# First FFN: down products two slices behind the gated products in all batches; scan: later weight loads, shift and root in steps of their own

## The chip, the cores and the metric

The kernel runs on one core of a Trainium2 chip. The metric is the device time of one launch in microseconds. TensorE (PE, with its weight loads as PEld), VectorE (DVE), ScalarE (ACT), GpSimd (POOL) and the queue of SyncE (SP) work side by side and meet through semaphores.

## The reference

Two blocks of a sequence model, in float32, on four batches of 512 tokens with 512 channels. What the change touches is the first FFN, then the scan of the second block, and the entry of the last attention, of which batch 0 is prepared inside the scan.

```python
x = x + _L0_attn_ref(_layernorm(x), W_qkv, W_o)
x = x + _L0_ffn_ref(_layernorm(x), w1, w3, w2)
x = x + _L1_attn_ref(_layernorm(x), W_xproj, W_dt, b_dt, A_log, D_param)
x = x + _L1_ffn_ref(_layernorm(x), ...)

def _L0_ffn_ref(x, w1, w3, w2):          # w*q: weights rounded to three values
    g = silu(x @ w1q.T) * (x @ w3q.T)    # hidden size 1365
    return g @ w2q.T

def _L1_attn_ref(x, W_xproj, W_dt, b_dt, A_log, D_param):
    ...
    def step(h, inp):                    # 512 tokens, 512 channels, 16 states
        h = dA_t * h + Bu_t
        y = jnp.sum(h * C_t[:, None, :], axis=-1)
        return (h, y)
    ...

def _L1_ffn_ref(x, ...):                 # latent attention, then a mixture of experts
    h = x + attention(rmsnorm(x, ln1_w), kv_d_w, q_d_w, k_u_w, v_u_w, ...)
    return h + moe(rmsnorm(h, ln2_w), ...)
```

## The kernel before

The residual rows stay in SBUF (`xs[b]`, one tile per batch). The stages follow one another: first attention, first FFN, scan, second attention, experts. Two of them matter here.

**First FFN** (the loop over `b` and the 11 slices `f` of the hidden size; the last slice has 85 rows). `gated(b, f, ...)` makes one slice: sixteen matmuls into `pg`, a tile of the PSUM tag "pair" with two buffers of two banks (L844), then silu on ACT (L849), the product with the other half on DVE (L850), a rounded copy `gh` on ACT (L855) and the rest `gl` on DVE (L856). `gh` and `gl` have `GBUFS` = 3 buffers each. `down(b, f, ...)` multiplies a finished slice with `w2` into the four banks `ys` (eight matmuls, L862); the first of a batch begins with the first finished slice that leaves `pending`. After the last slice what is left in `pending` is multiplied, and DVE adds `ys` to `xs[b]` (L914). The list `pending` holds the slices whose down product is not yet issued; it may hold `lag` of them, 2 in batch 0 and 1 in the others.

Between these products the loop calls `part(n)` three times a slice: in the middle of the gated products, after them, and after the down product. In batches 1 to 3 a part advances `prepare(b - 1, ...)`, which makes the scan's inputs of the batch before: layer norm rows (`row_s`, L123), their products on POOL (L590, L591), transposes `tp` into a half of a "pair" buffer with a copy to `uT` on ACT (L132, L133), the projections `pb`, `pd`, `pz`, the softplus on ACT and DVE (L635 to L649), and transposes `tpd` of `ux` (L657). Later parts also advance `inputs(b + 1)`, which makes the next batch's `hTh` and `hTl` through transposes `tpf` (L826 to L833). Parts 2, 3 and 5 advance nothing. Part 0 is the layer norm, part 1 makes rows 0 and 1, part 4 is the transpose of row 0, part 6 that of row 1. In this stage only PE's order is that of the text (`manual_schedule`); the order on DVE, ACT, POOL and SP, and the buffer that a tile takes, are chosen by the framework's planner.

**Scan** (128 steps `m`: batch, state `n`, half). Here the order on all engines is that of the text. A step issues, in this order: DVE's addition of the batch before (`finish`, at `m % 32 == 3`), a part of `between` (the last batch's preparation, drained at `m` = 84), a part of `come` from `m` = 85 on, at even steps `scale` for the next `n` (a `diag` load on SP, three `bu` rows L1103 and four decays `da` L1109 on ACT), the first turn of the next step on PE (L1116, L1121), the two scans on DVE (L1129), `weigh` on POOL (`hc`, L1140, at even steps with a `cb` load on SP, L1137), `add_up` of step `m - 3` on PE (L1153) and the second turn. PSUM has eight banks: four hold the sums `ys`, the turns and the parts share the others.

At `m` = 84 the pool of the last batch's preparation is closed, its room is given to the tiles of the later stages, and a list `loads` is filled: 14 loads on SP and one memset of `wr` on POOL, in the order `ln1`, `wlat` twice, `wrk` (the profile's `w_b`), `wup` three times, `wku`, `cos1`, `sin1`, `wow`, `ln2`, the memset, `wr`, `br`. From `m` = 86 each step issues one. In steps 91 to 94 ACT scales a quarter of `wlat` and of `wrk` by `ln1` (L1248).

`come` is `enter(0, c1, 1)`; its argument `apart` is 1 only here (for the other batches `enter` runs in the second attention with `apart` = 0). A step runs it to its next `yield`. Before the change its parts are: steps 85 to 88 one token slice's statistics each on DVE (L108, L109), in 88 also `root_inverse` (a `tensor_scalar` on DVE, L102, and a power on POOL, L103); step 89 the shift on DVE (L150) and the first shifted row with its square and sum on ACT (L155, L1015); steps 90 to 92 the other three, in 92 also the second `root_inverse`; steps 93 to 98 the rows `row_d` (ACT, L1028), their transposes (PE, L1032) and the copies to `hT` (ACT, L1023); from step 99 `enter_singly`, which begins with the products `pl` of `wlat` and `hT` (L956), two matmuls a step.

Of the kernel before, what the change touches and what calls it, by code (L numbers as in the profile page):

```python
# [22 lines left out]
NK = C // P  # L23
# [6 lines left out]
GBUFS = 3  # L30
# [16 lines left out]
def block_kernel(ctx: ExitStack, tc: tile.TileContext, a: dict, out: bass.AP):  # L47
# [50 lines left out]
    def root_inverse(pool, v, eps, scale, name):  # L98

        shape = list(v.shape)  # L100
        r = pool.tile(shape, F32, tag="ri_" + name, name="ri_" + name)
        nc.vector.tensor_scalar(r, v, scale, eps, ALU.mult, ALU.add)  # L102
        nc.gpsimd.tensor_tensor(r, r, minus_half[:, : shape[1]], ALU.pow)  # L103
        return r
# [42 lines left out]
    def shift_of(pool, mv, rs):  # L147

        shift = pool.tile([P, NT], F32, tag="shift", name="shift")
        nc.vector.scalar_tensor_tensor(shift, mv[:, :, 0], -1.0, rs, ALU.mult, ALU.mult)  # L150
        return shift
# [635 lines left out]
    with tc.tile_pool(name="b_s", bufs=1) as bs, tc.tile_pool(name="b_1", bufs=1) as b1, tc.tile_pool(  # L787
# [3 lines left out]
        def quantize_down(f):  # L791
            rows = FROWS[f]
            raw = b2.tile([P, C], F32, tag="row", name="q_w2")[:rows]
            nc.sync.dma_start(raw, a["w2T"][f * P : f * P + rows, :])
            ternary(b2, w2[:rows, f, :], raw, scales["w2"], C)

        def clear():
            zero = b2.tile([P, C], F32, tag="sil", name="zero")
            nc.vector.memset(zero, 0.0)
            nc.gpsimd.dma_start(acc[B * T :, :], zero)  # L800
# [66 lines left out]
        with tc.manual_schedule(engines={mybir.EngineType.PE}):  # L867
            for _ in inputs(0, first_mv):
                pass
            for f in range(3):  # L870
                quantize_down(f)
            for b in range(B):
                hT = high_low.pop(b)
                between = prepare(b - 1, bs, half_pair, halves, 2) if b > 0 else iter(())
                coming = inputs(b + 1) if b + 1 < B else iter(())
                ys = None

                light = [False]

                def part(n):
                    if n % 3 == 2 and n > 3 * 4 and b + 1 < B:
                        next(coming, None)
                        if not light[0]:
                            return
                    if n not in (2, 3, 5):
                        light[0] = next(between, False)


                lag = GBUFS - 1 if b == 0 else 1
                pending = []
                for f, rows in enumerate(FROWS):
                    pending.append((f, rows, gated(b, f, rows, hT, lambda: part(3 * f))))
                    if b == 0 and f + 3 < NF:
                        quantize_down(f + 3)
                    if b == 0 and f == 6:
                        clear()
                    part(3 * f + 1)  # L900
                    if b == B - 1 and f == 0:
                        for _ in fetch(0):
                            pass
                    if b == 0 and f == 4:
                        scan_constants(b2)
                    if len(pending) > lag:
                        if ys is None:
                            ys = [bank(f"y{t}") for t in range(NT)]
                        down(b, *pending.pop(0), ys)
                    part(3 * f + 2)  # L910
                for job in pending:
                    down(b, *job, ys)
                for t in range(NT):
                    nc.vector.scalar_tensor_tensor(  # L914
                        xs[b][:, t, :], ys[t], scales["w2"][:, 2:3], xs[b][:, t, :], ALU.mult, ALU.add
                    )
# [84 lines left out]
    def enter(b, pool, apart=0):  # L1001


        mv = pool.tile([P, NT, 2], F32, tag="mv", name="mv_d")
        for t in range(NT):
            statistics(pool, xs[b], t, mv)
            if t == NT - 1:
                rs = root_inverse(pool, mv[:, :, 1], LN_EPS, 1.0, "ln")
            yield
        shift = shift_of(pool, mv, rs)  # L1010
        ss = pool.tile([P, NT], F32, tag="ss", name="ss_d")
        for t in range(NT):
            shifted(hs[b][:, t, :], xs[b], t, rs, shift)
            sq = pool.tile([P, C], F32, tag="row", name="sq_d", bufs=2)
            nc.scalar.activation(sq, hs[b][:, t, :], AF.Square, accum_out=ss[:, t : t + 1])  # L1015
            if t == NT - 1:
                rs = root_inverse(pool, ss, RMS_EPS, 1.0 / C, "rms")
            yield
        hT = far.tile([P, NK, T], F32, tag="hT", name="hTd")
        before = tp = None  # L1020
        for t in range(NT + 1 + apart):
            if tp is not None:
                nc.scalar.copy(hT[:, :, (t - 2) * P : (t - 1) * P], tp.rearrange("p (k q) -> p k q", k=NK))  # L1023
                tp = None
            row = None
            if t < NT:
                row = pool.tile([P, C], F32, tag="row", name="row_d", bufs=2)
                nc.scalar.activation(row, hs[b][:, t, :], AF.Copy, scale=rs[:, t : t + 1])  # L1028
            if before is not None and apart:
                tp = bank("tp")  # L1030
                for k in range(NK):
                    nc.tensor.transpose(tp[:, k * P : (k + 1) * P], before[:, k * P : (k + 1) * P], ident)  # L1032
            elif before is not None:
                transpose_into(hT, before, (t - 1) * P)
            before = row
            yield
        if apart:
            yield from enter_singly(b, pool, hT)
            return
        lat = d1.tile([P, 2, T], F32, tag="lat", name="lat")  # L1040
        for i in range(2):
            pl = bank("pl")
            for k in range(NK):
                nc.tensor.matmul(
                    pl, wlat[:, k, i, :], hT[:, k, :], start=k == 0, stop=k == NK - 1
                )
            nc.scalar.copy(lat[:, i, :], pl)
        yield
        v = d2.tile([P, NT, C], F32, tag="v", name="vd")
        both = turned_pair()  # L1050
        rows = {}
        for t in range(NT + 2):
            if t >= 2:
                done = rows.pop(t - 2)
                for s, scale in enumerate((SCALE, 1.0)):
                    transpose_into(
                        both[s], done[:, s].rearrange("p h d -> p (h d)"), (t - 2) * P, scale
                    )
            if t < NT:
                tok = slice(t * P, (t + 1) * P)  # L1060
                pv = bank("pvd")
                nc.tensor.matmul(pv, lat[:, 0, tok], wup[:, 0, :], start=True, stop=True)
                nc.scalar.copy(v[:, t, :], pv)

                pq = pair("pqd")
                nc.tensor.matmul(pq[:, 0, :], lat[:, 1, tok], wup[:, 1, :], start=True, stop=True)
                nc.tensor.matmul(pq[:, 1, 0 : H * RD], lat[:, 0, tok], wku, start=True, stop=True)
                for k in range(NK):
                    nc.tensor.matmul(
                        pq[:, 1, H * RD :], hT[:, k, tok], wrk[:, k, :],  # L1070
                        start=k == 0, stop=k == NK - 1,
                    )
                qk = rows[t] = d2.tile([P, 2, H, D], F32, tag="qk", name="qkd")
                rot = d1.tile([P, 2, H, RD], F32, tag="rot", name="rotd")
                for s in range(2):
                    rotate(qk, rot, pq[:, s, :], t, s)
                nc.gpsimd.tensor_tensor(qk[:, :, :, RD:], qk[:, :, :, RD:], rot, ALU.add)
            if t < NT + 1:
                yield
        ready[b] = both + (v,)  # L1080
        yield

    eight("s")
    with tc.tile_pool(name="c_1", bufs=1, reuse_waits="tile") as c1, tc.tile_pool(
# [83 lines left out]
        with tc.manual_schedule(engines=engines):  # L1168
            coming, loads = iter(()), []
# [3 lines left out]
            for m, (b, n, half) in enumerate(steps):  # L1173
# [27 lines left out]
                if m == 84:  # L1201
# [38 lines left out]
                    loads.append(lambda: nc.gpsimd.memset(wr, 0.0))  # L1240
                    hold(wr[:, :, :NR], by_rows(a["router_w"]))
                    hold(br, a["router_b"].partition_broadcast(P))
                if m >= 86 and loads:
                    loads.pop(0)()
                if 91 <= m < 91 + NK:
                    k = m - 91
                    for w in (wlat[:, k].rearrange("p i r -> p (i r)"), wrk[:, k]):
                        nc.scalar.activation(w, w, AF.Copy, scale=ln1[:, k : k + 1])  # L1248
            for step in steps[-3:]:
# [60 lines left out]
    with tc.tile_pool(name="d_1", bufs=1) as d1, tc.tile_pool(name="d_2", bufs=2) as d2, tc.tile_pool(  # L1310
# [146 lines left out]
        with tc.manual_schedule(engines={mybir.EngineType.PE}):  # L1457
# [5 lines left out]
            for m in range(n + 4):  # L1463
                b, at = divmod(m, each)
# [358 lines left out]
```

## Time and profile before

| | us |
|---|---|
| median of 3 runs | 1855.8 (1854.12 to 1862.17) |
| profiled execution, whole | 1858.7 |
| its span, first to last instruction | 1857.0 |
| first attention | 0 to 428 |
| first FFN | 428 to 733 |
| scan | 733 to 1100 |
| second attention | 1100 to 1535 |
| experts | 1535 to 1857 |

Over the span PE is busy 94%, DVE 64%, ACT 51%, POOL 31%. The mean granted clock of TensorE is 0.98. Busy shares over the whole span mix stages with different limits; the prediction therefore reads one stage at a time. In the lines that it shows, "[x <-Y]" after an instruction is the time for which its engine sat idle before it, and the instruction that ended that wait. Times of lines in the order of time are from the start of the span.

### The profile page before, as it was taken

To read this page: it belongs to the slowest core of one execution; us is meant where nothing else is said; L and a number is where in the kernel's file an instruction comes from. 1 tells how busy PE (TensorE), PEld (TensorE's weight loads), DVE (VectorE), ACT (ScalarE), POOL (GpSimd) and SP (SyncE) were. 2 spreads that over 40 slices of the span, in tenths; PEclk is the share of its full clock that TensorE was granted. 3 is DMA by queue.
4 is the path that set the end of the run, shared out by engine and by line. 5 is a ranking of instruction groups with operands and counts; after the bars stand their busy time and mean duration, and the time that the engine had idled before them with its cause. 6 is when DMAs were issued, how large, how long until landed. Compare 5 with 4: busy or idle time off the path is not lost.

```text
span 1857.0 us, 27575 instructions
## 1 busy us (share of the span) xinstructions
PE 1740.2 (94%) x10374; PEld 1093.0 (59%) x10374; DVE 1186.6 (64%) x1908; ACT 938.0 (51%) x1940; POOL 581.5 (31%) x383
## 2 busy tenths in 40 slices
PE   7899899989999998989997989999999999999998
PEld 3443344437777676878886875556556554544444
DVE  6577757786655556899887886574766764322222
ACT  2433533332242536889988867576676652111111
POOL 2231313120202021889887860100000000244431
PEclk9999999999999999999999988999999999999999
DMA  7002300102011112333223200000010006455545
GB/s 244 22 1 68 109 1 1 46 1 76 5 40 53 59 56 82 94 92 102 58 73 102 58 28 1 1 24 1 1 35 24 24 24 230 150 91 91 91 79 142
DMA packets 74630, 115.07 MB, mean 62 GB/s; under 512 B 9546, under 2 KB 34762, under 8 KB 73940
## 3 DMA queue, kind: packets, MB, share of 16 engines
q1 hardware_dynamic: 64996, 90.87, 15.4%
q0 software_dynamic: 8656, 20.32, 6.1%
q10 hardware_dynamic: 848, 2.13, 0.3%
q8 instruction: 83, 1.36, 0.3%
q14 instruction: 47, 0.39, 0.1%
HBM read 83.02 MB, written 33.42 MB: 63 GB/s over the span
## 4 chain that ended last, share of the span: by engine, by line
PE 68%; DVE 13%; ACT 11%; issue 3%; DMA 3%; POOL 1%; DVEq 0%; SPq 0%; ACTq 0%; POOLq 0%
PE pgr L1702 7%; PE pg L844 6%; PE pq L284 5%; PE ys L1153 4%; PE yr L1723 4%; PE scd L1387 4%; PE bu L1121 3%; PE y L1327 3%; PE y L862 3%; PE pge L1288 3%; PE tp L132 3%; PE bu L1116 3%; PE y L340 3%; PE tpd L1410 2%; ACT pr L1398 2%
## 5 line engine op out<-in xcount | busy, mean ns | idle before, releaser
L1140 POOL TENSOR_TENSOR hc<-h,cb 128x1024 f32<-128x1024 f32 x128 | 301.1, 2378 | 115.4 <-DVE h L1129 93.7
L1129 DVE TENSOR_TENSOR_SCAN h<-da,bu 128x512 f32<-128x512 f32 x256 | 295.1, 1204 | 28.5 <-PE bu L1121 14.3
L284 PE MATMUL pq<-wqkv,hT 128*128 128x512 f32 x384 | 179.6, 615 | 4.8 <-DVE qk L300 3.6
L1109 ACT ACTIVATE da<-delta_l,am 128x511 f32<-128x511 f32 x256 | 163.4, 709 | 2.1 <-DVE h L1129 2.0
L1398 ACT ACTIVATE pr<-scd,nm 128x128 f32<-128x128 f32 (+3 forms) x256 | 133.3, 530 | 57.6 <-DVE nm L1395 56.7
L844 PE MATMUL pg<-hTh,w 128*128 128x512 f32 (+1 forms) x352 | 145.6, 414 | 1.0 <-ACT hTh L831 0.7
L844 PE MATMUL pg<-hTl,w 128*128 128x512 f32 (+1 forms) x352 | 139.9, 397 | 0.2 <-DVE hTl L832 0.2
L1153 PE MATMUL ys<-ident,hc 128*128 128x128 f32 x1024 | 136.7, 277 | 3.3 <-DVE h L1129 1.7
L1121 PE MATMUL bu<-ident,bu 128*128 128x128 f32 x768 | 132.2, 279 | 6.4 <-ACT bu L1103 6.4
L1702 PE MATMUL pgr<-wgu,gTe 128*128 x304 | 137.1, 593 | 0.0
L1103 ACT ACTIVATE bu<-dxT,bts 128x512 f32<-128x512 f32 x192 | 124.3, 712 | 16.2 <-PE bu L1121 13.3
L284 PEld LDWEIGHTS pq<-wqkv,hT 128*128 128x128 f32 x384 | 71.5, 194 | 97.3 <-issue 91.2
L366 ACT ACTIVATE pt<-sc 128x1024 f32<-128x1024 f32 (+3 forms) x128 | 83.3, 698 | 78.0 <-PE sc L361 72.3
L1387 PE MATMUL scd<-kTd,qTd 32*128 32x512 f32 (+3 forms) x512 | 109.0, 507 | 14.0 <-ACT pr L1398 11.3
L1153 PEld LDWEIGHTS ys<-ident,hc 128*128 128x128 f32 x1024 | 119.0, 143 | 4.3 <-DVE h L1129 1.9
L1116 PE MATMUL bu<-diag_l,dxT 128*128 128x128 f32 x512 | 105.9, 289 | 16.3 <-DVE h L1129 13.3
L367 POOL TENSOR_SCALAR_AFFINE_SELECT pt<-pt 128x512 f32<-128x512 f32 x64 | 56.2, 879 | 179.1 <-ACT pt L366 156.5
L1395 DVE TENSOR_REDUCE nm<-scd 128x2 f32<-128x256 f32 (+3 forms) x128 | 105.0, 821 | 2.8
L1410 PE MATMUL tpd<-ident,pr 128*128 128x128 f32 x640 | 102.6, 290 | 3.5 <-ACT ptd L1417 1.1
L1116 PEld LDWEIGHTS bu<-diag_l,dxT 128*128 128x128 f32 x512 | 82.3, 196 | 40.0 <-DVE h L1129 23.2
L1121 PEld LDWEIGHTS bu<-ident,bu 128*128 128x128 f32 x768 | 95.6, 145 | 9.9 <-ACT bu L1103 9.9
L1709 DVE SCALAR_TENSOR_TENSOR hidr<-pgr,silr 128x256 f32<-128x256 f32 x38 | 16.1, 425 | 130.0 <-ACT silr L1707 130.0
(338 smaller groups left out, 3290.7 us busy)
## 6 DMA issues: line engine op xcount, KB each, us to landing
cb<-c_rows SPq DMA_DIRECT2D x64, 256.0 KB, 3.3
q_w<-in_w2T SPq DMA_DIRECT2D x20, 256.0 KB, 2.8
diag_l<-diags SPq DMA_DIRECT2D x64, 64.0 KB, 2.0
hrows<-h SPq DMA_DIRECT2D x4, 1024.0 KB, 4.3
acc<-x SPq DMA_DIRECT2D x16, 256.0 KB, 2.0
wgu<-in_r_gate SPq DMA_DIRECT2D x7, 512.0 KB, 9.5
wgu<-in_r_up SPq DMA_DIRECT2D x7, 512.0 KB, 10.0
wdn<-in_r_down SPq DMA_DIRECT2D x7, 512.0 KB, 9.3
```

The costliest lines, as they stand in the source:

```text
L284: nc.tensor.matmul(y, inputs_T[b][:, k, t * P : (t + 1) * P], wqkv[:, k, s * C : (s + 1) * C], start=k == 0, stop=k == NK - 1,)
L844: nc.tensor.matmul(pg[:rows, i, :], w[:, k, f * P : f * P + rows], part[:, k, :], start=k + m == 0, stop=k + m == NK,)
L1109: nc.scalar.activation(da[:, k, 1:], delta[:, k, 1:], AF.Exp, scale=am[:, k, n : n + 1])
L1116: nc.tensor.matmul(bu[:, :P], loaded[b][1][:, 0, k * P : (k + 1) * P], scaled[b, n][0], start=True, stop=True,)
L1121: nc.tensor.transpose(bu[:, t * P : (t + 1) * P], scaled[b, n][t][:, k * P : (k + 1) * P], ident)
L1129: nc.vector.tensor_tensor_scan(h[:, i, :], decays[b, n][:, 2 * half + i, :], bu, 0.0, ALU.mult, ALU.add)
L1140: nc.gpsimd.tensor_tensor(hc, states.pop((b, n, half)), weighed[b, n].unsqueeze(1).to_broadcast([P, 2, T]), ALU.mult)
L1153: nc.tensor.matmul(sums[b][t][:, k * P : (k + 1) * P], hc[:, i, t * P : (t + 1) * P], ident, is_transpose=True, start=n == 0 and k == 0, s ...
L1387: nc.tensor.matmul(sc[:, i, :w], qT[at, g, t * P : w], kT[at, g, :w], start=True, stop=True)
L1398: nc.scalar.activation(pr[:, i, :w], sc[:, i, :w], AF.Exp, bias=nm[:, i : i + 1], accum_out=sums[b, g][:, t, 2 * p + i : 2 * p + i + 1],)
L1410: nc.tensor.transpose(tp[:, j * P : (j + 1) * P], pr[:, i, j * P : (j + 1) * P], ident)
L1702: nc.tensor.matmul(pg, gT[:, k, :], wgu[:, bass.ds(e, 1), k, :].rearrange("p e o -> p (e o)"), start=k == 0, stop=k == NK - 1,)
```

## The change

In the first FFN `lag` becomes `GBUFS - 1` = 2 in every batch. In `enter`, where `apart` is set, the statistics take two token slices a part, the shift gets a part of its own, and so does the second `root_inverse`; the number of parts stays eight, so `hT`'s rows still begin at step 93. With `apart` = 0 nothing changes. In the scan the loads begin at step 91 instead of 86 and the scalings of `wlat` and `wrk` at 95 instead of 91.

The parts of steps 85 to 92 after the change: two statistics; two statistics and the first root; the shift; four times a shifted row with its square; the second root.

```diff
-                lag = GBUFS - 1 if b == 0 else 1
+                lag = GBUFS - 1
...
             if t == NT - 1:
                 rs = root_inverse(pool, mv[:, :, 1], LN_EPS, 1.0, "ln")
+            if not apart or t % 2 == 1:
+                yield
+        shift = shift_of(pool, mv, rs)
+        if apart:
             yield
-        shift = shift_of(pool, mv, rs)
         ss = pool.tile([P, NT], F32, tag="ss", name="ss_d")
         for t in range(NT):
             shifted(hs[b][:, t, :], xs[b], t, rs, shift)
...
             if t == NT - 1:
+                if apart:
+                    yield
                 rs = root_inverse(pool, ss, RMS_EPS, 1.0 / C, "rms")
             yield
...
-                if m >= 86 and loads:
+                if m >= 91 and loads:
                     loads.pop(0)()
-                if 91 <= m < 91 + NK:
-                    k = m - 91
+                if 95 <= m < 95 + NK:
+                    k = m - 95
```

## The prediction

> **What bounds the kernel now.** I read the stretches of the stages first, then PE's waits in the first FFN, then the order of time on each engine where PE waits. The columns of a stretch are its length, busy time and instructions of PE, weight loads, DVE, ACT and POOL, granted clock, DMA share, GB/s.
>
> ```profile
> 428.00:733.00 305.00, 293.89 (x1356) 222.89 (x1356) 178.50 (x280) 120.62 (x173) 40.20 (x30) 0.99 0.16 51
> 733.00:1100.00 367.00, 336.15 (x2568) 299.09 (x2569) 325.89 (x326) 321.38 (x532) 309.50 (x138) 0.97 0.27 79
> ```
>
> The first row is the first FFN, the second the scan. In the FFN only PE is full: 11.1 of 305 us are idle. In the scan four engines are near their limit; between 1006 and 1099 us PE is busy 91.98 of 93.00. So in both a wait of PE is lost time, unless PE would wait later for the same chain anyway. PE's waits in the FFN (total us, times, longest):
>
> ```profile
> PE y L862 <- DVE gl L856: 4.3, 8, 1.2
> PE y L862 <- ACT gh L855: 2.0, 2, 1.7
> PE tpd L657 <- DVE ux L652: 1.3, 2, 0.7
> ```
>
> The first two, 6.3 us, are what a larger lag can remove. By place: 1.16 and 1.06 at the first down product of batches 1 and 3; 0.30, 0.30, 0.77 in mid-batch; 0.34, 1.87, 0.58 at the last down product of batches 1, 2, 3. The one of batch 2 also costs clock (third figure from the end):
>
> ```profile
> 648.02:651.43 3.41, 1.97 (x7) 1.42 (x8) 1.61 (x3) 1.10 (x2) 0.00 (x0) 1.00 0.85 262
> 651.43:654.84 3.41, 3.41 (x9) 2.64 (x8) 3.41 (x8) 0.00 (x0) 0.00 (x0) 0.50 0.94 320
> ```
>
> PE idles 1.44 us of the first stretch and works at half clock in the second: 1.7 us lost.
>
> **Part 1, lag 2 in batches 1 to 3.** No instruction is added; a down product (eight matmuls, 1.85 us) moves behind the next gated product (sixteen, 3.73 us).
>
> Removed: at the starts 1.16 + 1.06 = 2.2. At the ends down(10) now has two down products ahead of it. gl(10) is ready 3.1, 4.6 and 2.9 us after gated(10), PE comes after some 4, so 0.34 and 0.58 go and 0.5 of 1.87 stays: 2.3. With it goes the half clock, 1.7.
>
> Counted at nothing: the mid-batch 1.37. Behind each, tpd waits for DVE (0.66, 0.67, 1.15) at the end of a chain on ACT and DVE that began earlier; PE only comes there sooner. Without that cover 1.4 more is gained.
>
> Added: down(0) stood between gated(1) and gated(2); now only a transpose (tp) does, and the PSUM pair has two buffers, one held by pg(1), one by tp. In batch 2 gated(1) ends and tp starts at 579.71, and PE is free at 580.06:
>
> ```profile
> 579.97 0.69 ACT L849 ACTIVATE sil<-pg,sc_w 128x512 f32<-128x512 f32 x1 [1.66 <-PE pg L844]
> 580.55 0.59 ACT L133 ACTIVATE uT<-tp 128x512 f32<-128x512 f32 x1
> 581.65 1.62 DVE L123 TENSOR_SCALAR row_s<-x,mv,ri_ln 128x512 f32<-128x512 f32 x1 [1.19 <-POOL ud L590]
> 583.20 0.74 DVE L850 SCALAR_TENSOR_TENSOR sil<-pg,sc_w,sil 128x512 f32<-128x512 f32 x1
> ```
>
> tp's buffer is free at 581.14, pg(1)'s only at 583.94: L850 is queued behind a row that waits for POOL. That a buffer comes free as a whole, after L850, is seen elsewhere; this weight load waits for an L850 that ended at 542.81:
>
> ```profile
> 542.07 0.74 DVE L850 SCALAR_TENSOR_TENSOR sil<-pg,sc_w,sil 128x512 f32<-128x512 f32 x1
> 542.86 0.19 PEld L844 LDWEIGHTS pg<-hTh,w 128*128 128x128 f32 x1 [0.36 <-DVE sil L850]
> ```
>
> Today gated(2) starts at 504.20, 582.26 and 664.32, each time before that L850 ends, so it takes tp's buffer. If it still does, it waits 1.1, 1.15, 1.1; the next transpose, in its middle, takes pg(1)'s buffer and waits 0.7, 0.95, 0.6. Together 5.6. If it takes pg(1)'s instead, 3.7, 3.9, 3.6: 11.2. I take 5.6, since the copy that frees tp's buffer comes first. Each start then has 1.7 to 2.1 us of idle PE within 4 us; a window with 1.44 idle lost the clock, the one from 975.69 with 1.92 did not. Bounds 0 and 3 × 1.7; I take one, 1.7.
>
> The Trainium skill ("TensorE: Matmul & The Clock Gate", section "HAM oscillation") puts the bound at "no PE-idle gaps >~3.4µs". By it the 1.7 that is removed and the 1.7 that is added are both zero, with the same sum here; the trace disagrees at 651.43, where a gap of 1.65 was enough.
>
> Waiting for gh buffers is not added: three buffers, and down(f-3) is issued before gated(f). FFN: -2.2 -2.3 -1.7 +5.6 +1.7 = +1.1.
>
> **Part 2, the scan.** Around steps 85 to 98, the places where an engine waits for another:
>
> ```profile
> 976.85 1.68 DVE L102 TENSOR_SCALAR ri_ln<-mv_d 128x4 f32<-128x4 f32 x1
> 980.85 0.81 ACT L155 ACTIVATE h<-x,shift,ri_ln 128x512 f32<-128x512 f32 x1 [4.02 <-DVE shift L150]
> 991.92 0.17 DVE L102 TENSOR_SCALAR ri_rms<-ss_d 128x4 f32<-128x4 f32 x1 [4.42 <-ACT sq_d L1015]
> 993.27 0.79 PE L1116 MATMUL bu<-diag_l,dxT 128*128 128x128 f32 x2 [3.77 <-DVE h L1129]
> 1005.23 0.66 PE L1032 MATMUL tp<-ident,row_d 128*128 128x128 f32 x4 [2.55 <-ACT row_d L1028]
> ```
>
> ACT, some three steps ahead, stops 4.02 us for the shift, queued on DVE behind scan(88). It is then behind: DVE waits for its fourth square, PE for row_d, and ACT has no pause until 1020.
>
> After the change, DVE, from 966.82: two statistics (0.82 each), scan(85) until 970.75, two statistics, L102. L102 took 1.68 while POOL multiplied (it ended at 978.53, hc at 978.51) and 0.17 with POOL idle; hc(85) now runs from 970.9 to 973.3, so I end L102 there. Scan(86) ends at 975.6, the shift at 975.7, ACT's first shifted row starts at 975.85. ACT is free from 972.44, so it idles 3.4 instead of 4.0. The saving is small because the first shifted row now stands before the scaling for n = 13 (4.4 us), which used to fill ACT while DVE got there. That scaling ends at 981.7 instead of 976.8; scan(90) needs its half at about 980.4 and comes at 982.4: hidden, with 2 us of cover. Then ACT: four rows with squares at 1.47, scalings 4.4 and 4.3, until 990.45 instead of 991.8. DVE still idles 3.6.
>
> The Trainium skill ("SBUF — State Buffer", section "SBUF: two separate sides") calls the port pair of DVE and GpSimd "an exclusive lock", which is the 1.68 row; by the 0.17 row the shift would come 0.8 us sooner and the scan's gain be 3.5 rather than 2.7.
>
> From there to the third row_d: scaling 4.35, two rows 1.3, scaling 4.35, copy 0.5, row 0.65, that is 1001.6 instead of 1005.1, since three pairs of weight scalings (0.8 each) left the way. PE, there at about 1001.2, waits 0.6 with the latency instead of 2.55. The pairs return behind it: 0.8 + copy and row 1.15 + scaling 4.35 + 0.8 + 0.5 + 0.8 + 0.5 puts the last hT copy at 1010.5, so PE's first pl comes at 1010.6 instead of 1014.0, after about 1 us of waiting. The fourth pair follows another scaling (1015.8); the second pl, in step 100, waits 0.3 for it. Step 101's pl: 1018.7 instead of 1021.38. **Scan: -2.7.** PE is full from there to 1099, so it stays. Bounds: all of PE's waits from 977 on and the half clock at 1006.41 gone, -11.3; the three later pairs all on PE's way, +2.4.
>
> The queues: SP's 15 issues move five steps back, past two or three pairs of diag and cb. SP's wait of 5.5 us ahead of ln1 (for DVE's ux) goes; it cost nothing, as the diag behind it was issued at 969.38 for a product near 979. w_b, issued in step 94, leaves SP at about 986 and lands 6.7 us later, nine ahead of ACT; if SP were ten later, ACT and all behind it would wait 1. wr waits on SP for a memset in POOL's queue, 15.1 us today; in its new place the next cb is one step further off: nothing.
>
> **Sum.** +1.1 - 2.7 = -1.6. The profiled execution took 1858.7 (span 1857.0 and 1.7 around it), which gives 1857.1; it lies 2.9 above the median 1855.8, so on the median's footing **1854**. A measurement of this kernel tells about 0.5% (9.3 us) from no change.
>
> **Rivals.**
> *The starts don't wait* (DVE takes L850 ahead of the row, or the planner places buffers otherwise): FFN -2.2 - 2.8 - 1.4 - 1.7 = -8.1, with the scan -10.8: **1845**. For: batch 0 runs lag 2 without such waits. Against: it has no prepare between its slices. 0.25.
> *Slower: gated(2) waits for pg(1)'s buffer.* 11.2 instead of 5.6, and each gap of 3.6 to 3.9 halves the clock, 5.1 instead of 1.7: +9.0, total +7.4: **1863**; with nothing from the scan 1866. For: L850 ends 4 us after gated(1). Against: tp's buffer was taken so far. It decides from 3.0 us a batch (8.9 / 3), where it eats all that is removed. 0.22.
> *It all comes back* before the stages end, or ACT's pause only moves: **1856**. For: DVE and POOL are 89 and 84% busy in the scan. Against: PE has no idle after 1006. 0.08.
> The forecast, 1848 to 1860, has 0.45. Faster by over 0.5%: nearly all of the first rival, 0.25; slower: the upper half of the second and a mishap in DVE's unwritten order, 0.17; within: 0.58. The range, 1844 to 1865, reaches to both.
>
> **What would show it.** pg L844 waiting about 1.1 us at slice 2 of batches 1 to 3, released by ACT (by DVE: the second rival); no wait of y except some 0.5 at batch 2's end; ACT idle 3 to 4 us before the first shifted row; PE's 2.55 before row_d under 1. Wrong if y's waits stay, if ACT's pause goes, or if PE idles after step 101.

## The result, and the profile after

The changed kernel takes 1850.73 us (median of 20 runs), the kernel before 1855.63 beside it: a ratio of 0.9976, 95% interval 0.9966 to 0.9986, or 4.5 us less (2.6 to 6.3). That is a real gain and under the 0.5% that was set as the bound. A second set of 5 runs gave 0.9961 (0.9949 to 0.9974).

The profiled execution was a good one of its kind: 1848.07, span 1846.2, against 1858.7 and 1857.0 before. The 10.8 us between the spans are not all of the change. 3.7 lie in the first attention, which is the same program: 2.3 of them are there by 66 us, ahead of the first half-clock window (3.41 us at a granted clock of 0.50) that either profile records, at 74.6 and 186.8, and the rest comes and goes where such windows fall. Another 1.9 lie between the FFN's end and step 84 of the scan, where the change does nothing either. I therefore compare stretches, each from an instruction to an instruction. First the kernel before, the first FFN (first gated matmul to last down matmul) and the scan from the first scan of step 84 to that of step 101:

```profile
428.25:731.53 303.28, 293.85 (x1355) 222.84 (x1355) 177.11 (x279) 118.96 (x170) 40.03 (x29) 0.99 0.16 51
962.94:1020.25 57.31, 45.47 (x336) 40.58 (x335) 47.06 (x50) 51.69 (x92) 41.78 (x20) 0.94 0.34 100
```

The same two of the changed kernel:

```profile
424.56:726.22 301.66, 292.11 (x1355) 223.10 (x1355) 179.93 (x279) 119.66 (x171) 39.58 (x29) 0.99 0.16 51
955.70:1009.08 53.38, 44.39 (x336) 39.04 (x335) 46.00 (x50) 48.71 (x87) 42.77 (x20) 0.97 0.38 110
```

The FFN is 1.6 us shorter, the middle of the scan 3.9. From step 101 to step 127 both take 73.90: what the scan wins by step 101 it keeps. PE's waits in the FFN of the changed kernel (total us, times, longest):

```profile
PE pg L844 <- ACT uT L133: 2.7, 3, 0.9
PE tpd L657 <- DVE sil L850: 2.3, 1, 2.3
PE pg L844 <- DVE sil L850: 1.8, 3, 0.7
PE tpd L657 <- DVE ux L652: 1.4, 2, 0.7
PE tp L132 <- DVE sil L850: 1.2, 3, 0.5
...
```

No wait of y for gh or gl is left, 6.3 us before. In their place stand the three waits for the copy to uT and the three of tp for L850, at slice 2 of batches 1 to 3, as forecast, and longer waits of pg and tpd in mid-batch. This is the start of batch 2 in the order of time, PE first, then ACT, then DVE:

```profile
577.35 0.50 PE L844 MATMUL pg<-hTh,w 128*128 128x512 f32 x1 [0.89 <-ACT uT L133]
...
579.85 0.66 PE L132 MATMUL tp<-ident,row_s 128*128 128x128 f32 x4 [0.36 <-DVE sil L850]
...
576.71 0.59 ACT L133 ACTIVATE uT<-tp 128x512 f32<-128x512 f32 x1
...
577.61 1.52 DVE L123 TENSOR_SCALAR row_s<-x,mv,ri_ln 128x512 f32<-128x512 f32 x1
579.05 0.74 DVE L850 SCALAR_TENSOR_TENSOR sil<-pg,sc_w,sil 128x512 f32<-128x512 f32 x1
```

The copy ends at 577.30 and gated(2) starts at 577.35: it took tp's buffer. L850, behind a row on DVE, ends at 579.79, and the next transpose starts at 579.85: it took pg(1)'s.

The scan of the changed kernel, where an engine waits for another (its lines from `enter` on stand three to five further down than before):

```profile
965.14 0.90 DVE L102 TENSOR_SCALAR ri_ln<-mv_d 128x4 f32<-128x4 f32 x1
968.36 0.81 ACT L155 ACTIVATE h<-x,shift,ri_ln 128x512 f32<-128x512 f32 x1 [3.07 <-DVE shift L150]
982.93 0.17 DVE L102 TENSOR_SCALAR ri_rms<-ss_d 128x4 f32<-128x4 f32 x1 [3.48 <-ACT sq_d L1018]
987.86 0.33 PE L1037 MATMUL tp<-ident,row_d 128*128 128x128 f32 x1 [1.31 <-ACT row_d L1033]
993.85 0.33 PE L1037 MATMUL tp<-ident,row_d 128*128 128x128 f32 x1 [0.66 <-ACT row_d L1033]
1002.58 0.70 PE L956 MATMUL pl<-hTd,wlat 128*128 128x512 f32 x1 [0.84 <-ACT hTd L1028]
```

ACT's stop for the shift is 3.07 (forecast 3.4, 4.02 before), DVE's before the second root 3.48 (3.6, 4.42), PE's for the third row 0.66 (0.6, 2.55), its wait for the last hT copy 0.84 (about 1, none before). The wait for the first row, 1.31, was not forecast; it was 0.73 before.

### The profile page after: what moved, and what is told of

The parts are those of the page before. It is cut to its first block, busy times and chain, and to the rows that moved or that the text cites. A ratio compares the mean times of both kernels' runs of the same rounds, so it can differ in the third digit from the quotient of the medians.

```text
span 1846.2 us, 27566 instructions
## 1 busy us (share of the span) xinstructions
PE 1733.0 (94%) x10374; PEld 1090.2 (59%) x10374; DVE 1188.1 (64%) x1908; ACT 937.9 (51%) x1940; POOL 581.2 (31%) x383
## 3 DMA queue, kind: packets, MB, share of 16 engines
q8 instruction: 83, 1.36, 0.3%
## 4 chain that ended last, share of the span: by engine, by line
PE 68%; DVE 14%; ACT 11%; issue 3%; DMA 2%; POOL 1%; SPq 0%; DVEq 0%; ACTq 0%; POOLq 0%
PE pgr L1707 7%; PE pg L844 6%; PE pq L284 5%; PE ys L1158 4%; PE scd L1392 4%; PE yr L1728 4%; PE y L862 3%; PE bu L1126 3%; PE y L1332 3%; PE pge L1293 3%; PE tp L132 3%; PE bu L1121 2%; PE tpd L1415 2%; PE y L340 2%; ACT pr L1403 2%
```

## The experiments

Ratios are to the kernel before, timed beside each group.

**The two parts apart.** First the FFN's part alone:

```diff
-                lag = GBUFS - 1 if b == 0 else 1
+                lag = GBUFS - 1
```

> Lag 2 in all batches, the scan as before. Theory (two parts that add up): the first FFN shortens by the 1.6 us that the two traces show (first gated matmul to last down matmul 303.3 to 301.7), time 0.999 of before; PE waits 0.9 for the copy of tp and some 0.4 before the next transpose at slice 2 of batches 1 to 3, and nowhere for gh or gl. Rival (only the scan part counts): ratio 1.000, the new waits eat all that is removed.

Measured: 0.9988 (0.9977 to 0.9999), 2.2 us less. The waits of the FFN are those of the changed kernel within 0.3 us, with one wait for gl of 0.2 at the end of batch 2. Then the scan's part alone, that is the change without this line.

> The scan's part of the change alone, lag as before. Theory: 2.9 us less, ratio 0.9984; the FFN keeps its 6.3 us of waits for gh and gl; ACT stops 3.1 instead of 4.0 for the shift and PE waits about 0.7 instead of 2.55 for the third row. Rival (the FFN carries the gain): ratio 1.000.

Measured: 0.9991 (0.9981 to 1.0002), FFN waits of y 5.0 us (6.3 expected), steps 84 to 101 in 53.38. The product of the two ratios is 0.9979; the change has 0.9976. By these medians each part carries about half. The intervals are as wide as the effects, and the second includes 1.000, so that by time its rival does not fall. Both rivals fall by the traces: the old waits of the FFN are gone in the first, and the scan's stretch is shorter in the second.

The first of these runs also shows what the clock does to a stretch. It has the scan of the kernel before, and steps 84 to 101 took 55.76 there against 57.31. Both have two half-clock windows there. Before, the second began at 1006.41, where PE is full; the stretch is 1.55 us longer, of at most 1.7 that 3.42 us at half clock can cost. In this run the two stand at 989.1 to 995.9, at the end of a wait of PE for DVE and ahead of one for ACT's third row; that row ends 42.25 us after step 84 (42.23 before), and PE's wait for it only got shorter, 1.85 for 2.55. The old scan's stretch in this run:

```profile
959.72:1015.48 55.76, 45.10 (x336) 40.04 (x335) 46.94 (x50) 50.13 (x89) 41.87 (x20) 0.94 0.35 103
```

The new scan took 53.37 or 53.38 in all five profiles that have it unchanged. So the scan's part is worth 2.4 us where the old scan's windows fall well, and 3.9 where they don't.

The FFN shows the same. Its batches 1 to 3, from the first gated matmul of batch 1 to the last down matmul of batch 3, took 236.45 us with the old lag in the one profile without a half-clock window there, and 237.10 to 241.06 in the three others; with lag 2 they took 235.05 to 235.89 in three profiles without a window and 236.59 and 237.16 in two with one. Here is the one without a window with the old lag (from the run with `enter` alone, below), and one of lag 2 (the changed kernel again); the granted clock is 1.00 in both:

```profile
491.25:727.70 236.45, 227.76 (x1068) 170.00 (x1066) 138.40 (x210) 100.15 (x141) 38.62 (x27) 1.00 0.16 53
490.65:726.21 235.56, 226.11 (x1068) 170.26 (x1066) 139.25 (x210) 101.02 (x142) 38.43 (x27) 1.00 0.16 53
```

So by these profiles the waits alone are worth 0.6 to 1.4 us. The rest of the FFN's gain goes with the windows: four fell there in four profiles with the old lag, two in five with lag 2. That the waits for gh and gl bring the windows on is argued from their place, not shown by a run of its own.

**The two halves of the scan's part.** Loads and weight scalings only:

```diff
-                if m >= 86 and loads:
+                if m >= 91 and loads:
...
-                if 91 <= m < 91 + NK:
-                    k = m - 91
+                if 95 <= m < 95 + NK:
+                    k = m - 95
```

> Only the loads from step 91 and the weight scalings from 95; statistics, shift and roots as before. Theory: the weight scalings on ACT's way are most of the scan's gain: ACT still stops 4.0 for the shift, DVE's wait before the second root falls from 4.4 to 3.6, PE's wait for the third row from 2.55 to under 0.5; about -2 us. Rival (the parts of their own carry it): about 0.

Measured: 0.9993 (0.9984 to 1.0001); steps 84 to 101 in 54.35. Its waits from step 84 on:

```profile
ACT h L155 <- DVE shift L150: 4.0, 1, 4.0
...
DVE ri_rms L102 <- ACT sq_d L1015: 3.6, 1, 3.6
...
PE tp L1032 <- ACT row_d L1028: 0.7, 1, 0.7
```

And `enter` alone as changed, with loads from 86 and scalings from 91:

> Only the parts (two statistics a step, shift and second root in steps of their own); loads from 86, scalings from 91. Theory: ACT stops 3.1 instead of 4.0, the fourth square ends 1.7 earlier (one scaling pair now behind it), but all four pairs still stand before the third row, so that PE waits some 1.6 for it instead of 2.55; about -1 us. Rival: the whole -2.9.

Measured: 0.9995 (0.9983 to 1.0006); steps 84 to 101 in 54.79. Its waits:

```profile
ACT h L155 <- DVE shift L150: 3.1, 1, 3.1
...
DVE ri_rms L102 <- ACT sq_d L1018: 3.5, 1, 3.5
...
PE tp L1037 <- ACT row_d L1033: 3.2, 2, 2.5
```

Against 55.76 the loads save 1.4, the parts 1.0, together 2.4, which is what both have. By time neither is told from no change, so these sizes are those of one profile each. The stops of ACT and DVE in the first are as expected; PE's wait is 0.7 where under 0.5 was expected. In the second the last wait is a miss: the third row ends 0.95 us earlier after step 84 (41.28 for 42.23 us), but PE comes earlier by as much and still waits 2.55.

**Where the new waits of the FFN come from.** The first transpose moves behind the start of gated(2), and part 12 ("step 12" in the expectation) advances the preparation twice:

```diff
-                    if n not in (2, 3, 5):
+                    if n not in (2, 3, 4, 5):
+                        light[0] = next(between, False)
+                    if n == 12:
                         light[0] = next(between, False)
```

> The changed kernel, but the first transpose of the preparation moves from behind gated(1) to the middle of gated(2), so that both PSUM pairs are not taken when gated(2) starts; each later transpose follows one part later and two parts share step 12. Theory (the new waits come from the pair's two buffers): PE's waits at slice 2 of batches 1 to 3, 0.89 x 3 and 0.36 to 0.47, go; FFN 3 to 4 us shorter than in the changed kernel, ratio to the kernel before about 0.9958. Rival (they come from DVE's order, the row ahead of L850): the wait only moves to the transposes, no gain against the changed kernel (0.9976).

Measured: 0.9954 (0.9940 to 0.9968), 1847.57 us. Its waits in the FFN:

```profile
PE pg L844 <- DVE sil L850: 2.1, 4, 0.7
...
PE tp L132 <- DVE sil L850: 0.7, 1, 0.7
```

The three waits for uT are gone, so the two buffers of the pair made them. L850 is still late at that place and shows once before tp (0.66) and twice before pg (0.36, 0.35). Batches 1 to 3 took 234.07 us, against 236.59 in the changed kernel; both have one half-clock window there. The edit is worth 2.5 us by this pair. Where no window fell, in the run with two edits below, they took 232.28 against 235.05 to 235.89, which is 2.8 to 3.6 less; 3 to 4 were expected.

In the other test down(0) stays behind gated(1), and the lag grows at slice 3:

```diff
-                    if len(pending) > lag:
+                    if len(pending) > (lag if b == 0 or f > 2 else 1):
```

> The changed kernel, but in batches 1 to 3 down(0) is again issued behind gated(1), and the second slice of lag is taken at slice 3. Theory: at the starts PE waits for gl again (1.2 and 1.1 in batches 1 and 3) instead of 3.9 in all for the pair's buffers; the ends stay free of waits: 1.5 us less than the changed kernel, ratio about 0.9968. Rival (the waits at the start come with lag 2 wherever it is taken): a wait of 0.9 + 0.4 shows at slice 4 instead.

Measured: 0.9970 (0.9956 to 0.9983), which doesn't tell it from the changed kernel; batches 1 to 3 took 238.19 us with one window, not less but 1.0 to 1.6 more than the two profiles of lag 2 with one. Two of its waits:

```profile
PE pd L615 <- ACT bts L556: 2.5, 3, 0.8
PE y L862 <- DVE gl L856: 2.4, 3, 1.2
```

The waits for gl are back, as expected, and those for the pair don't move to slice 4, so the rival falls too. But at both places tried the slice without a down product takes 1.85 us of cover from what PE issues next: here pd, which is released by ACT's copy to bts, 0.83 late in each batch. Lag has a price at the place where it is taken up, and by the traces slice 2 was the cheaper of the two.

**What binds the scan.** ACT makes the inputs for n = 13 (the scaling: bu rows and decays) ahead of the first shifted row:

```diff
-                if m > 84:
+                if m > 84 and m != 88:
                     next(come, None)
...
                         coming = fetch(b + 1)
+                if m == 88:
+                    next(come, None)
```

> The changed kernel, but in step 88 ACT does the scaling for n = 13 before the first shifted row, so that it has work while DVE gets to the shift. Theory (ACT's stop for the shift is passed on to DVE and PE): the stop of 3.1 goes, DVE's wait before the second root falls from 3.5 to 0.5, PE's waits for row_d (1.3, 0.7) and for hT (0.8) nearly go; 2 to 3 us less than the changed kernel, ratio about 0.9962. Rival (DVE or POOL bound the scan there anyway): 0.9976.

Measured: 0.9971 (0.9958 to 0.9985); steps 84 to 101 in 52.02, 1.36 less than in the changed kernel; the time alone does not tell it from that kernel. Its waits:

```profile
DVE ri_rms L102 <- ACT sq_d L1018: 2.1, 1, 2.1
...
PE pl L956 <- ACT hTd L1028: 0.8, 1, 0.8
```

ACT's stop is gone and PE waits for no row any more, but about half of the expected gain was missed. The decays have two buffers; the scaling for n = 13 writes the one that the scans of steps 86 and 87 read, and waits three times for them, 1.24 us in all. And the wait of pl for the last hT copy stays: two pairs of weight scalings (wlat and wrk) stand just before it.

The second root behind the scans of step 92, in the changed kernel:

```diff
-                if m > 84:
+                if m > 84 and m not in (92,):
                     next(come, None)
...
                 scan(b, n, half)
+                if m == 92:
+                    next(come, None)
                 weigh(b, n, half)
```

> The changed kernel, but the second root of step 92 is issued behind that step's two scans instead of ahead of them, so that DVE has work while ACT finishes the fourth square. Theory (ACT is what binds from step 88 to 99, DVE's stop of 3.5 is only its echo): DVE's stop shrinks to about 1.2, PE's wait for DVE's scan behind it (1.5) goes, but the rows, the last hT copy and PE's first pl come when they came; steps 84 to 101 stay at 53.4 us, ratio 0.9976. Rival (DVE's stop is itself on the path): 2 us less, steps 84 to 101 at 51.

Measured: 0.9967 (0.9955 to 0.9979); steps 84 to 101 in 53.37. DVE's longest waits are now:

```profile
DVE h L1134 <- PE bu L1126: 3.0, 4, 1.5
DVE h L1134 <- ACT hTd L1028: 1.0, 1, 1.0
```

DVE's stop before the root is gone altogether; in its place DVE waits 3.0 us for PE's turns (0.5 in the changed kernel) and 1.0 for ACT's copy (0.7), and the stretch stays the same to 0.01 us. The stop was an echo of ACT, on an engine that is 87% busy in this stretch.

The late transpose and the scaling ahead of the first shifted row together; then both with the late root as well; then the changed kernel again:

> Both of these edits on the changed kernel. Theory: they add up, 6 us less than the changed kernel, ratio to before about 0.9944. Rival: each is eaten by the other stage's waits, no better than the better of the two.

> The changed kernel with the first transpose later, the scaling for n = 13 ahead of the first shifted row, and the second root behind the scans of step 92. Theory: with ACT's stop gone, its decays waited 1.2 for DVE, and DVE 2.1 for the fourth square; with the root later both go: steps 84 to 101 at 51 us or less (52.0 without the last edit), ratio about 0.9943. Rival (PE's way to the last hT copy binds): 52.0 again.

> The changed kernel once more, beside these two, so that they can be set against it on the same chip: 0.9976 of before.

Measured: 0.9949 (0.9936 to 0.9961) for two, 0.9945 (0.9931 to 0.9959) for three, 0.9961 (0.9949 to 0.9974) for the changed kernel beside the latter (1846.87 for three against 1849.61 us, six and five runs). Steps 84 to 101 took 52.01 with two edits and 52.00 with three: the third edit adds nothing here either, its theory fell and the rival's 52.0 came. What binds is ACT, more than PE: from the first shifted row to the last hT copy ACT has no stop over 0.15 us in these profiles, and PE's first pl starts 0.05 us after that copy's end. The two edits add up in the trace: 232.28 us for batches 1 to 3 and 52.01 for this stretch. By time two edits are faster than the kernel before, clear of noise. Against the changed kernel the gain is 5.0 us by its first ratio, 0.9976, and 2.2 by its second, 0.9961, whose interval overlaps; 6 were expected.

## Why the prediction was right, and where its sums were off

Forecast was 1.6 us less, measured 4.5 (2.6 to 6.3): the likeliest case, and the right side, but too small by 3 us. The FFN's part had the wrong sign: the sum had it 1.1 us longer, the traces have it 1.6 shorter. That the total came out on the right side rests on the scan's term. The range, 1844 to 1865, would have held for no change as well, so that it tests little.

*Removed in the FFN, forecast 2.2 and 2.3.* All waits of y went, and they were dearer than the list says. At the start of batch 1, before:

```profile
500.83 0.48 PE L862 MATMUL y<-w,gh 128*128 128x512 f32 x1
502.48 0.51 PE L862 MATMUL y<-w,gl 128*128 128x512 f32 x1 [1.16 <-DVE gl L856]
```

Matmuls of this kind are issued every 0.23 us; here 1.65 lie between two, so 1.42 are lost, and the list has 1.16, because it counts from the modelled end of the first. Counted from issue to issue, the waits of y cost 8.8 us instead of 6.4; there are eleven, one of them, 0.12, too short for the list. The waits that I *added* were worked out from the instant at which PE could issue. The step that failed is this mixture: what goes was measured with one ruler, what comes with another. At the starts and ends 6.8 us were removed by issue, where the sum had 4.5.

*Added, forecast 5.6.* By issue the three waits of pg cost 1.13 each and those of tp 0.5 to 0.6, 5.1 in all: right. The list shows 3.9 for the same.

*Mid-batch waits, counted at nothing.* They went, and came back: tpd in batch 3 waits 2.30 instead of 1.15, pg behind tpf 0.71 instead of 0.13 and 0.12. About right: 2.0 gone by issue and 2.3 returned.

*Clock at the starts, forecast 1.7.* None: of 15 starts in the five profiles with this FFN none lost the clock. No half-clock window falls at batch 2's end any more, as forecast; with the old lag three of four profiles have it. In two of those five profiles another came, behind the 2.30 us of batch 3:

```profile
702.20:705.61 3.41, 1.42 (x9) 1.25 (x10) 3.41 (x7) 1.93 (x4) 0.00 (x0) 1.00 0.42 158
705.60:709.02 3.42, 3.42 (x10) 2.67 (x9) 1.64 (x3) 0.69 (x1) 0.00 (x0) 0.50 0.68 226
```

Two us idle in one window were enough; in the run of the FFN's part alone 1.88 of the same wait fell in one window, and none followed. The Trainium skill's rule ("TensorE: Matmul & The Clock Gate", section "HAM oscillation") speaks of gaps over 3.4 us; the trace disagrees again, at 2.30.

By issue the FFN's sum is -8.8 + 5.1 + 2.3 = -1.4 without the clock, where I had +1.1 with it. That is the failed term; the stretches without windows differ by 0.6 to 1.4, and the run of this part alone gave -2.2 (-4.3 to -0.2), with the windows as they fell.

*The scan, forecast -2.7.* About right: -2.4 where the old scan's windows cost nothing that the trace shows, -3.9 against the profile before, whose window at 1006.41 only the lower bound counted. The chain was as forecast: the last hT copy ends 46.8 us after step 84 (forecast 47.6). L102 ended at 966.04, as POOL's multiplication did at 966.01, which agrees with "an exclusive lock" in the Trainium skill ("SBUF — State Buffer", section "SBUF: two separate sides").

*The slower rival*, that gated(2) waits for pg(1)'s buffer, fell: it is released by ACT's copy at all three starts. *The faster rival*, no waits at the starts, did not come, but the run with the late transpose shows most of it: 0.9954.

## What to carry to other kernels

Count a wait that you remove and one that you add in the same unit, from issue to issue; a list of idle times that starts at modelled ends is too short by a quarter of a microsecond for each wait here. A deeper lag removes the waits at its far end and uncovers whatever stands where it is taken up: look there for what the moved product was hiding. Where several engines are near their limit, take an engine's stop away before counting it as a loss: of DVE's 3.5 us 3.0 came back as other waits and nothing was gained; taking away ACT's 3.1 gained 1.4.

## What was not expected of the hardware

The half-clock windows fall differently from run to run, and the same old scan took 55.76 and 57.31 us between the same two steps, the longer where a window fell on a full PE. Idle time in a window doesn't decide alone: 1.44 us of idle were enough in the FFN, 1.92 in the scan (from 975.69, before) were not. The 13 profiles bound it. All 90 full-clock windows in which PE idled more than 1.92 us were followed by one at half clock, and none of those in which it idled less than 0.79; of the 429 between, 56 were. What else decides there wasn't tried.
